# Four layers of a graph network on one core: eight sums per batch moved from GpSimd to VectorE

## The chip, the cores and the metric

The kernel runs on one core of a Trainium2 chip. The metric is the device time of one execution in microseconds (us). The core has TensorE (PE) for matrix products, VectorE (DVE) and GpSimd (POOL) for elementwise work, ScalarE (ACT) for activations and copies, and SyncE (SP), whose queue issues nearly all transfers here. Each engine takes its instructions in order and waits at an instruction until what it needs has been signalled.

## The reference

For each of 32 independent batches there are 512 nodes with 128 features, x, and a 512x512 matrix adj. Four layers follow each other. Each first normalises x over its features, applies relu, and adds the layer's result to x. Cut to what matters:

```python
h = max(layernorm(x), 0);  x = x + L0(h, adj)     # scaled adj + eye, one product, leaky relu
h = max(layernorm(x), 0);  x = x + L1(h, adj)     # adj @ in_rep and adj.T @ out_rep, tanh
h = max(layernorm(x), 0);  x = x + L2(h, adj)
h = max(layernorm(x), 0);  x = x + L3(h, adj)     # one product with adj, then gates

# L2 repeats this layer four times, on the same adj:
src_agg = einsum('bjv,bij->biv', nodes @ ws + bs, l2norm(adj, axis=2))
dst_agg = einsum('bjv,bji->biv', nodes @ wd + bd, l2norm(adj, axis=1))
out = tanh(concat([src_agg, nodes @ wn + bn, dst_agg]) @ wu + bu)
```

All arrays are fp32.

## The kernel before

**Tiles.** A matrix lies in SBUF as 128 partitions x 4 chunks x 512 columns. Each batch holds it twice: `a` is adj, `aT` its transpose, both loaded by SP. Layers 0 and 1 use them as they are. For layer 2 both are scaled in place: eight multiplications `L1100` per batch (four chunks of `aT`, four of `a`) with the inverse norms, which arrive by a transfer in `rows`.

**Seven products in place of eight.** In layer 2 every product with a scaled matrix is formed from blocks of half its size in the manner of Winograd's variant of Strassen's scheme: seven block products and some sums in place of eight block products. On the side of the matrices the sums are made once a batch for all four inner layers. That is `made_of(m)`, called for `aT` and for `a`: four subtractions each, on operands of 128 partitions x 2 x 256 elements. Three write the new tile `made` (parts 1, 0 and 2), one overwrites half of the chunks 0 and 2 of the matrix itself, so it must follow the part 1 that reads the old ones. These eight subtractions per batch are the ones that the change moves. All go through the helper `summed`, whose one line, L777, records them together with other sums: `st` (on the side of the features), and `p`, `to`, `de`, `ge`, which combine products in PSUM. The profile's groups are told apart by tiles, not by that line.

**Order.** Nothing is issued in the order of the text. Every operation is recorded with its engine, an estimate of its duration, and what it reads and writes. `Plan.order` then replays them: for each engine it takes, of the operations that are ready, the one with the smallest key (a due time from the batch's number less the longest path behind the operation), and the result is the fixed order of each engine's queue. The third argument of `summed` is that estimate; in the part that the change touches it is 1.6 us, for GpSimd. `kept_warm` then puts filler products (`ps_idle`) into TensorE's queue where the planned gap is over 0.7 us. Two or three batches are under way at once, so that one's layer 2 fills TensorE while others pass through their chains.

**Names that the steps use.**
- `sc` (L662): the power -1/2 of the variance, on GpSimd; `nb` (L670), on VectorE, follows it; `h` (L674), on ACT, is the normalised input.
- `inv` (L1081): the same power for the inverse norms of layer 2.
- `blk`, `turn_turned`, `turned`: a transposition over DRAM. VectorE transposes blocks of 32x32 (L683), SP writes four pieces (L692) and reads them back (L696). ACT makes `hT` or `f` of it (L730), or VectorE adds it to x (`xr`, L711). Batches 0, 1 and 31 transpose on TensorE instead (`ps_t`; `xr` is L708 there).
- `ps_agg`: products of unscaled matrices; `ps_sd`: the two projections of an inner layer, which VectorE moves to `sd` (L763), whereupon `st` is formed; `ps_ab`, `ps_cd`: the products of inner layers 0, 2 and 3; `ps_a`, `ps_b`, `ps_c`: those of inner layer 1, combined into `ge`, which `ps_second` multiplies; `ps_msg`: layer 3's first product, of `hT`.
- `t_sb` (L441): ten differences of weight columns, once, in the start.

Of the kernel before, what the change touches and what calls it, by code (L numbers as in the profile page):

```python
# [19 lines left out]
B, N, D = 32, 512, 128  # L20
# [261 lines left out]
def gnn_stack(  # L282
# [11 lines left out]
    nc = tc.nc  # L294
# [27 lines left out]
    def t_tt(n, pointers=0):  # L322
        return 0.065 + 0.058 * pointers + n / 960
# [13 lines left out]
    def op(*args, **kwargs):  # L337
        return plan.op(*args, **kwargs)
# [118 lines left out]
    def program(b):  # L457
        plan.batch = b

        def buf(tag, shape=(P, N), name=None):  # L460
            return plan.buf(tag, shape, name)
# [311 lines left out]
        def two(m, k, j):  # L773
            return lambda: m.ap().rearrange("p (q k) n -> p q k n", k=2)[:, :, k, j * H:(j + 1) * H]

        def summed(engine, eng, us, o, x, y, sign, reads, writes):
            op(engine, us, lambda: eng.tensor_tensor(o(), x(), y(), op=ALU.subtract if sign < 0 else ALU.add), reads, writes)  # L777
# [4 lines left out]
        def made_of(m):  # L782


            tm, even, odd = buf("s6", (P, 2, 3, H), "made"), {0, 2}, {1, 3}

            def t(k):
                return lambda: tm.ap()[:, :, k, :]

            for o, x, y, reads, writes in (  # L790
                    (t(1), two(m, 1, 1), two(m, 0, 1), [m], [(tm, {1})]),
                    (two(m, 0, 1), two(m, 0, 1), two(m, 0, 0), [(m, even)], [(m, even)]),
                    (t(0), two(m, 1, 1), two(m, 0, 1), [m], [(tm, {0})]),
                    (t(2), two(m, 1, 0), t(0), [(m, odd), (tm, {0})], [(tm, {2})])):
                summed("POOL", nc.gpsimd, 1.6, o, x, y, -1, reads, writes)
            return tm

        def right(m, tm, k, pair):
# [227 lines left out]
        z, y = buf("s2", name="z"), buf("s2", name="y")  # L1026
# [79 lines left out]
        f = f0  # L1106

        made = [made_of(m) for m in (aT, a)]
        for i, (wsd, wn) in enumerate(W_L2):
            f_new = buf("s2", name=f"f{i + 1}")  # L1110
# [99 lines left out]
```

## Time and profile before

| what | us |
|---|---|
| median of 3 runs | 2358.41 |
| lowest and highest of them | 2356.08, 2361.54 |
| the profiled execution | 2359.71 |
| its span in the profile | 2357.9 |

| engine | busy, us | share of the span |
|---|---|---|
| TensorE | 2275.6 | 97% |
| VectorE | 1810.0 | 77% |
| ScalarE | 1183.5 | 50% |
| GpSimd | 562.4 | 24% |

The busy time of an engine is an average over stages. A group of the profile reads: line, engine, operation, output<-inputs, shape, count; then busy us and mean ns of one; then the engine's idle time before these instructions and what ended most of it. Each product of 512 columns appears as four records of TensorE, since it is issued in two halves of 64 columns and each half is recorded twice. The granted TensorE clock is 0.996 of full speed.

The eight sums appear as six groups on GpSimd, 256 instructions with 358.7 us of busy time in all; the shortest of them lasts 1256 ns.

### The profile page before, as it was taken

The numbers are of one execution on the slowest core, as the hardware profiler recorded it, in microseconds if no ns is written. First come the engines' busy times: TensorE is split into PE (matmuls) and PEld (weight loads), VectorE is DVE, ScalarE is ACT, GpSimd is POOL, SyncE is SP. The second block draws the span as 40 slices with busy tenths as digits, with TensorE's granted clock in tenths as the row PEclk, the third lists the DMA queues.
The fourth block names the chain that finished last, engine by engine and source line by source line (L and its number), as shares of the span: only waits on it lengthen the run. The fifth ranks groups of instructions, "written<-read, shape, count | busy, mean of one in ns | idle before, by whom it ended". The sixth has DMA issues, their size and how long they took to land.

```text
span 2357.9 us, 48190 instructions
## 1 busy us (share of the span) xinstructions
PE 2275.6 (97%) x18380; PEld 1403.2 (60%) x18380; DVE 1810.0 (77%) x4592; ACT 1183.5 (50%) x2723; POOL 562.4 (24%) x459
## 2 busy tenths in 40 slices
PE   8999999999999999999999999999999999999999
PEld 6566665555655566655556655565555566555566
DVE  7766777888777878787877778887778787878664
ACT  6543555544555444555445555445555445554323
POOL 3321222222122221222221222221222212222200
PEclk9999999999999999999999999999999999999999
DMA  6121343444343444333443434433434443333211
GB/s 241 37 82 51 112 125 107 125 132 120 101 121 109 134 123 124 110 118 112 129 120 106 129 103 129 131 118 103 122 110 133 123 124 109 117 109 114 72 47 58
DMA packets 199144, 264.48 MB, mean 112 GB/s; under 512 B 25984, under 2 KB 130688, under 8 KB 198912
## 3 DMA queue, kind: packets, MB, share of 16 engines
q1 hardware_dynamic: 198624, 261.26, 36.9%
q8 instruction: 145, 2.38, 0.4%
q14 instruction: 87, 0.71, 0.1%
q10 hardware_dynamic: 288, 0.13, 0.0%
HBM read 199.18 MB, written 62.13 MB: 111 GB/s over the span
## 4 chain that ended last, share of the span: by engine, by line
PE 61%; DVE 22%; DMA 7%; issue 3%; ACT 3%; POOL 2%; SPq 1%; DVEq 0%; ACTq 0%; POOLq 0%
PE ps_ab L823 20%; PE ps_cd L823 13%; PE ps_agg L354 8%; PE ps_sd L354 7%; DMA turned<-turn_turned 4%; DVE a L1100 4%; PE ps_seven L354 4%; DVE aT L1100 3%; DVE ge L777 3%; PE ps_gate L354 2%; PE ps_second L354 2%; PE ps_msg L354 1%; DVE st L777 1%; DMA turn_turned<-blk 1%; POOL sc L662 1%
## 5 line engine op out<-in xcount | busy, mean ns | idle before, releaser
L823 PE MATMUL ps_ab<-made,st 128*64 128x256 f32 x1536 | 412.2, 382 | 1.6 <-DVE st L777 1.6
L777 POOL TENSOR_TENSOR made<-aT 128x512 f32<-128x512 f32 x64 | 93.2, 1457 | 948.0 <-DVE aT L1100 835.6
L662 POOL TENSOR_TENSOR sc<-v,neg_half 128x4 f32<-128x4 f32 x127 | 148.7, 1177 | 547.9 <-DVE v L623 372.3
L354 PE MATMUL ps_sd<-w_sb,f 128*64 128x256 f32 x2048 | 265.8, 379 | 0.0
L823 PE MATMUL ps_ab<-aT,sd 128*64 128x256 f32 x768 | 226.5, 383 | 0.0
L823 PE MATMUL ps_cd<-aT,st 128*64 128x256 f32 x768 | 223.7, 381 | 1.4 <-DVE st L777 1.4
L823 PE MATMUL ps_ab<-a,sd 128*64 128x256 f32 x768 | 225.0, 381 | 0.0
L823 PE MATMUL ps_cd<-a,st 128*64 128x256 f32 x768 | 221.4, 383 | 0.0
L823 PEld LDWEIGHTS ps_ab<-made,st 128*64 128x64 f32 x1536 | 209.1, 138 | 12.5 <-DVE st L777 2.5
L354 PEld LDWEIGHTS ps_sd<-w_sb,f 128*64 128x64 f32 x2048 | 164.8, 137 | 68.6 <-issue 16.4
L674 ACT ACTIVATE h<-xr,nb,sc 128x128 f32<-128x128 f32 x384 | 162.3, 486 | 80.4 <-DVE nb L670 80.3
L823 PE MATMUL ps_ab<-made,sd 128*64 128x256 f32 x768 | 198.7, 381 | 0.0
L823 PE MATMUL ps_ab<-f,w_sb 128*64 128x256 f32 x768 | 190.1, 379 | 0.0
L886 ACT ACTIVATE f<-to,cf_sb 64x512 f32<-64x512 f32 x192 | 117.7, 613 | 142.8 <-DVE to L777 142.5
L763 DVE TENSOR_TENSOR sd<-ps_sd,rf_sb 128x512 f32<-128x512 f32 x192 | 123.6, 684 | 76.0 <-PE ps_sd L354 75.8
L823 PE MATMUL ps_ab<-ge,w_sb 128*64 128x256 f32 x512 | 144.0, 383 | 3.8 <-ACT f L886 1.6
L823 PEld LDWEIGHTS ps_ab<-aT,sd 128*64 128x64 f32 x768 | 105.4, 138 | 70.3 <-issue 27.7
L354 PE MATMUL ps_agg<-aT,rep 128*64 128x512 f32 x512 | 141.3, 598 | 1.3 <-DVE rep L1053 1.2
L354 PE MATMUL ps_agg<-a,rep 128*64 128x512 f32 x512 | 140.6, 592 | 0.0
L777 DVE TENSOR_TENSOR p<-p,ps_ab 64x256 f32<-64x256 f32 x192 | 81.3, 423 | 71.0 <-PE ps_ab L823 43.7
L1100 DVE TENSOR_TENSOR a<-a,rows 128x512 f32<-128x512 f32 x128 | 134.6, 1070 | 0.9 <-PE ps_agg L354 0.9
L354 PE MATMUL ps_agg<-aT,msg 128*64 128x512 f32 (+1 forms) x528 | 126.7, 580 | 0.0
(218 smaller groups left out, 5974.5 us busy)
## 6 DMA issues: line engine op xcount, KB each, us to landing
aT<-in_adjt SPq DMA_DIRECT2D x124, 512.0 KB, 7.0
turn_turned<-blk SPq DMA_DIRECT2D x696, 64.0 KB, 1.8
turned<-turn_turned SPq DMA_DIRECT2D x174, 256.0 KB, 2.7
a<-in_adj SPq DMA_DIRECT2D x62, 512.0 KB, 3.9
rows<-bounce SPq DMA_DIRECT2D x32, 512.0 KB, 4.5
shares<-bounce SPq DMA_DIRECT2D x32, 512.0 KB, 4.2
x<-in_x SPq DMA_DIRECT2D x32, 256.0 KB, 9.0
out<-xr SPq DMA_DIRECT2D x31, 256.0 KB, 3.2
```

Of the source, the lines that this page charges most:

```text
L354: nc.tensor.matmul(to[c], weight[:, c], data, start=start, stop=stop, skip_group_check=True)
L662: op("POOL", t_pow(n), lambda: nc.gpsimd.tensor_tensor(inv.ap()[:, :n], v8.ap()[:, :n], neg_half[:, :n], op=ALU.pow), [v8, NH], [(inv, {0})])
L674: op("ACT", t_act(D, 2), lambda c=c: nc.scalar.activation(h.ap()[:, c, :], xin.ap()[:, c, :], AF.Relu, bias=nb.ap()[:, c:c + 1], scale=inv ...
L763: op("DVE", t_tt(N), lambda ps=ps, h=h: nc.vector.tensor_add(sd.ap()[:, 2 * h:2 * h + 2, :], ps.ap().rearrange("p (j v) -> p j v", j=2), a ...
L777: op(engine, us, lambda: eng.tensor_tensor(o(), x(), y(), op=ALU.subtract if sign < 0 else ALU.add), reads, writes)
L823: nc.tensor.matmul(to(), lhs(), rhs(), start=start, stop=True, skip_group_check=True)
L886: op("ACT", t_act(n, 1), lambda: nc.scalar.activation(f_new.ap()[rows, cols], src(), AF.Tanh, bias=cf_sb[rows, i:i + 1]), reads + [(CF, {i ...
L1100: op("DVE", t_tt(N), lambda m=m, c=c, s=s: nc.vector.tensor_mul(m.ap()[:, c, :], m.ap()[:, c, :], rows.ap()[:, s, :]), [(m, {c}), rows], [ ...
```

## The change

The loop of `made_of` hands its four subtractions to VectorE's queue instead of GpSimd's, and the planner is given VectorE's estimate for one operation of 512 elements, `t_tt(N)`, 0.065 + 512/960 = 0.598 us, in place of 1.6. Operands and the loop's order are the same. As the planner works out all queues anew, other instructions change their places too.

```diff
             for o, x, y, reads, writes in (
                     (t(1), two(m, 1, 1), two(m, 0, 1), [m], [(tm, {1})]),
                     (two(m, 0, 1), two(m, 0, 1), two(m, 0, 0), [(m, even)], [(m, even)]),
                     (t(0), two(m, 1, 1), two(m, 0, 1), [m], [(tm, {0})]),
                     (t(2), two(m, 1, 0), t(0), [(m, odd), (tm, {0})], [(tm, {2})])):
-                summed("POOL", nc.gpsimd, 1.6, o, x, y, -1, reads, writes)
+                summed("DVE", nc.vector, t_tt(N), o, x, y, -1, reads, writes)
             return tm
```

## The prediction

> **What bounds the kernel now.** I read the shares first, then the waits of TensorE, then the two stretches in which its waits lie.
>
> ```profile
> PE 2275.6 (97%) x18380; PEld 1403.2 (60%) x18380; DVE 1810.0 (77%) x4592; ACT 1183.5 (50%) x2723; POOL 562.4 (24%) x459
> ```
>
> TensorE is busy 2275.6 of 2357.9 us. Time can only come out of its 82 us of idle time and of the filler products (ps_idle)[...]. The waits of TensorE (line, what it waited for: us in total, times, longest) place most of that:
>
> ```profile
> PE ps_msg L354 <- ACT hT L730: 39.2, 27, 2.6
> PE ps_second L354 <- DVE ge L777: 20.2, 28, 0.9
> PE ps_idle L354 <- DVE xr L708: 6.0, 1, 6.0
> ```
>
> The first two come once a batch: 1.45 + 0.72 = 2.2 us of a period of 70.8 us (L1100 aT starts at 1219.11 and again at 1289.94). The third is one stall in the start. The groups of VectorE, each shape apart, show something odd about the operation beside the sums:
>
> ```profile
> L1100 DVE TENSOR_TENSOR a<-a,rows 128x512 f32<-128x512 f32 x128 | 134.6, 1070 | 0.9 <-PE ps_agg L354 0.9
> L1100 DVE TENSOR_TENSOR aT<-aT,rows 128x512 f32<-128x512 f32 x128 | 86.5, 680 | 2.5 <-DMA rows<-bounce 1.4 <-PE ps_agg L354 1.0
> ```
>
> The same operation on the same shape takes 680 ns for aT and 1070 ns for a. The a ones run while GpSimd works on sums of aT. The timelines of GpSimd and VectorE around 1226 us show it (start, us, what):
>
> ```profile
> 1226.35 1.61 POOL L777 TENSOR_TENSOR aT<-aT 128x512 f32<-128x512 f32 x1
> ...
> 1225.53 2.98 DVE L1100 TENSOR_TENSOR a<-a,rows 128x512 f32<-128x512 f32 x2
> ...
> 1232.95 1.22 DVE L670 SCALAR_TENSOR_TENSOR nb<-mv,sc 128x4 f32<-128x4 f32 x1 [0.40 <-POOL sc L662]
> ...
> 1235.65 1.94 PE L354 MATMUL ps_second<-ge,w_sb 128*64 128x512 f32 x8 [0.70 <-DVE ge L777]
> ```
>
> Two multiplications that should start 0.60 us apart take 2.9 us, and a 128x4 operation with a median of 164 ns takes 1.22 us. VectorE is back to back from 1218.5 to 1236.7 but for that 0.40 us, so its loss reaches ge, and TensorE.
>
> In the start it is worse. The chain of waits over 20 to 70 us runs through the same victims:
>
> ```profile
> 37.59 4.57 DVE a L1100 x4
> 42.16 0.08 DVE v L991
> 42.24 6.68 DVE t_sb L441 x9
> ...
> 52.46 6.47 PE ps_idle L354 x72
> ```
>
> Nine 128x64 subtractions take 6.7 us beside the sums, where 128x128 ones of the same kind take 0.28 us each in the clear (L452 to L455).
>
> **What the Trainium skill says.** "SBUF — State Buffer", section "SBUF: two separate sides": VectorE with two SBUF inputs and a GpSimd operation that reads SBUF share a port pair under an exclusive lock; whoever starts first keeps it for the whole instruction, the other blocks. The trace agrees: one multiplication of a rises to at most 1770 ns, one sum on GpSimd lasts about 1270 ns, and the clean multiplication 680. "GPSIMD Engine Reference", section "Engine selection": two-input elementwise work is about 2x slower there than on VectorE. Here it is 1270 ns (clean) against 680. "VectorE: DVE Perf Modes", section "Why tensor_tensor can't do 2×_2P or 4×": an fp32 tensor_tensor has no fast mode, so I price a sum like a multiplication. The trace agrees for contiguous operands (680 ns, starts 0.60 us apart: four aT from 35.09 to 37.51); the sums' two runs of 256 are seen on no VectorE row, which I bound below.
>
> **The change part by part.** Per batch, eight sums of 128x512 leave GpSimd and enter VectorE.
>
> *Total load.* Added: 256 x 0.60 = 154 us of VectorE. Removed: the lock's loss, 128 x (1.070 - 0.680) = 50 us on a, 127 x (0.406 - 0.164) = 31 us on nb (L670), some 6 us on t_sb and 1 us on one y. VectorE goes from 1810 to about 1880 us, 80%. It does not become the bound as a whole; only the stretch counts. GpSimd keeps its powers (L662, L1081) and loses the queue before them. It issues no DMA. Loads of a and aT no longer wait for GpSimd before reusing a buffer; that was 1.3 us in the waits of SP, so nothing.
>
> *The start.* Before: L1100 begins at 35.09, and the first ps_sd<-f (layer 2) at 60.51. After, with the built program's order, in which the eight sums follow the multiplications at once and t_sb comes after:
>
> | step | ends at, us |
> |---|---|
> | aT and a, 8 x 0.60 | 39.9 |
> | 8 sums x 0.60 | 44.7 |
> | one t_sb, xr L708 | 45.6 |
> | 4 statistics, 4 aggregations, small ones | 47.1 |
> | power on GpSimd 1.0; meanwhile t_sb x7 and half of z; nb | 48.9 |
> | h on ACT, 4 x 0.40 | 50.5 |
> | turn on TensorE, copy on ACT | 51.4 |
> | ps_agg of batch 2 on TensorE, then ps_sd<-f | 52.6 |
>
> That is 7.9 us earlier, and 3.4 us of ps_agg that came after ps_sd<-f before now lie ahead of it (the order of TensorE shows both moves, and one filler group of 6 where groups of 36 and 8 stood). So 11.3 us less idle, of which I give back 1 us at the next step, where ps_cd waits for sd and st. **Start: -10 us**, bounds -5 and -13. As TensorE is full afterwards, what is saved here stays saved.
>
> *The steady batches.* The order repeats from about batch 5 to 29, 27 periods with its like around. In VectorE's queue six sums now stand ahead of blk<-h (the transpose that feeds hT) and two behind it. From 1225.53 to the end of blk<-h:
> - added: 6 x 0.60 = 3.6 us;
> - gone: 1.7 us on a (2.9 - 1.2), 1.1 us on nb (1.26 to the next start, against 0.16), 0.40 us waiting for GpSimd's power, which two sums and blk<-y now cover, and some 0.4 us of gaps between dependent neighbours that sums now separate;
> - sum: 3.6 - 3.6 = 0. blk<-h ends at about 1236.7, as before.
>
> What waits behind it on the SP queue is the read-back of turned (for y), which stands after the first two writes of blk<-h in both orders. So xr L711 (1240.94) does not move either, nor the sd and st after it (first st at about 1244.6).
>
> Two orders change. (1) ge: the first ps_second<-ge needs ge's half 0, finished by the third of four operations before, by the second now: 0.43 us earlier, so this stall falls from 0.70 to about 0.3. (2) TensorE: ps_msg stood first, waiting for hT; now ps_cd and ps_ab, 5 pairs x 0.43 = 2.2 us, stand ahead of it, and the first ps_cd waits for st instead. A wait takes the place of the one removed: ps_cd can start at about 1244.6, against 1245.01 before with a quarter of ps_msg (0.27) done by then. Gain over both stalls 0.15 to 0.2 us in the batch shown, whose waits sum to 1.82; the mean batch waits 2.2 us, the excess being hT's DMA, which the new order hides. I take **-0.3 us a batch, -8 us** in 27. Bounds: none of the waits left, -2.2; sums at 0.70 instead of 0.60, +0.3.
>
> The two sums behind blk<-h fill VectorE's 0.93 and 1.79 us waits for ps_second and turned; without that cover they would cost 1.2 us. made is first used at 1245.9, 8 us after the sums end. A later blk<-h of the next layer's h (behind z, y and xr now, about 1.9 us) still leaves f0 ready at about 1256, and ps_sd<-f takes it at 1257.3. Batches 30 and 31 and the end lose no wait that I price.
>
> Sum: -10 - 8 = -18 us on the profiled execution's 2359.7 (span 2357.9 and 1.8 around it), which stands 1.3 us over the median of 2358.4: 2341.
>
> **The rivals.**
> - *Only the start is won.* The stall at ps_cd takes all that ps_msg gave: -10, 2348. For it: blk<-h does not move. Against: ge's new order. Chance 0.20.
> - *VectorE gives it back: slower.* The stretch 1225 to 1237 is VectorE's bound, and each 0.1 us by which a sum is dearer delays ge and blk<-h by 0.6 us a batch. If the lock explained only half of the 2.8 us, the stretch would end 1.4 us later: 27 x 1.1 (after the 0.3) - 10 = +20, 2378. It decides from a net delay of 0.37 us a batch (10/27). For it: VectorE has no slack there. Against: aT is 680 ns in all 128 cases, and a's median is 685 with a long tail, as of blocking by chance of time. Chance 0.16, a third of it within 0.2%.
> - *Both waits vanish.* -10 - 27 x 2.2 = -69, 2290. Against: hT hangs on SP and DMA behind the same blk<-h. Chance 0.04.
> - *My forecast*, 2326 to 2346: 0.60.
>
> That the change does not do what it says can be excluded: the built order has the 256 sums on VectorE.
>
> **How the numbers follow.** The likeliest case gives 2341. Start bounds and steady bounds of +-0.4 us a batch make 2326 to 2355; beyond it lie most of the slower rival and the vanished waits. About 0.2%, 4.7 us, is what this measurement can tell from no change: faster 0.82 (forecast, start only, waits vanish, less the tail above 2353.7), same 0.07, slower 0.11.
>
> **What would show it.** Right: a<-a,rows at 680 like aT; nb near 164; made on VectorE at about 680 ns; ps_sd<-f near 52.6; TensorE's wait for ge about halved, for hT gone, and one for st in its place of under 1 us a batch. Wrong: sums over 750 ns, a still above 900, or waits for st, ge and sd together above 2.5 us a batch.

## The result and the profile after

The changed kernel takes 2339.05 us (median of 3 runs, 2338.88 to 2339.23) against 2358.41; the ratio is 0.9917, with a 95% interval of 0.9894 to 0.9939. Its profiled span is 2337.5 us, at a granted clock of 0.999. The page's shares:

```profile
PE 2273.1 (97%) x18304; PEld 1350.8 (58%) x18304; DVE 1839.8 (79%) x4848; ACT 1175.0 (50%) x2723; POOL 239.4 (10%) x203
```

TensorE does the same work but for 76 records of filler products; VectorE has 256 more instructions and only 30 us more busy time. The waits of TensorE (us in total, times, longest):

```profile
PE ps_cd L823 <- DVE st L777: 24.7, 27, 2.1
PE ps_second L354 <- DVE ge L777: 21.9, 27, 1.6
```

The wait of ps_msg for hT (39.2 us) is gone; one of ps_cd for st has taken its place; the wait for ge is still there (20.2 before). The groups of VectorE, each shape apart (busy us, mean ns of one, idle before):

```profile
L1100 DVE TENSOR_TENSOR a<-a,rows 128x512 f32<-128x512 f32 x128 | 86.4, 682 | 0.8 <-PE ps_agg L354 0.7
L1100 DVE TENSOR_TENSOR aT<-aT,rows 128x512 f32<-128x512 f32 x128 | 86.3, 680 | 1.5 <-PE ps_agg L354 0.9 <-DMA rows<-bounce 0.6
L777 DVE TENSOR_TENSOR made<-aT 128x512 f32<-128x512 f32 x64 | 43.7, 683 | 0.0
L670 DVE SCALAR_TENSOR_TENSOR nb<-mv,sc 128x4 f32<-128x4 f32 x127 | 20.3, 160 | 15.1 <-POOL sc L662 14.1
```

The multiplication of a has fallen from 1070 to 682 ns, the same as that of aT, and nb from 406 to 160. A sum lasts 683 ns, so its runs of 256 elements cost nothing extra.

**The start.** The timeline of VectorE from the last multiplications on (start, us, what):

```profile
38.98 2.66 DVE L1100 TENSOR_TENSOR a<-a,rows 128x512 f32<-128x512 f32 x4
41.55 0.68 DVE L777 TENSOR_TENSOR made<-aT 128x512 f32<-128x512 f32 x1
...
45.77 0.68 DVE L777 TENSOR_TENSOR made<-a,made 128x512 f32<-128x512 f32 x1
...
49.10 0.89 DVE L441 TENSOR_TENSOR t_sb<-w_sb 128x64 f32<-128x64 f32 x6
```

and that of TensorE:

```profile
54.77 2.33 PE L354 MATMUL ps_sd<-w_sb,f 128*64 128x256 f32 x20
```

Six subtractions t_sb take 0.89 us; nine took 6.68 before. The first ps_sd<-f starts 18.3 us after the first L1100 (36.52 in this run) instead of 25.4. Between 45 and 65 us TensorE's idle time and filler products come to 0.05 + 1.87 us, against 6.04 + 8.03 before: 12.2 us won.

**A steady batch.** VectorE in the dense stretch, from the variance v to nb; then GpSimd and TensorE:

```profile
1214.08 0.16 DVE L623 TENSOR_SCALAR v<-mv 128x4 f32<-128x4 f32 x1
1214.15 0.68 DVE L777 TENSOR_TENSOR made<-aT 128x512 f32<-128x512 f32 x1
1214.75 0.68 DVE L777 TENSOR_TENSOR a<-a 128x512 f32<-128x512 f32 x1
1215.35 0.70 DVE L683 STREAM_TRANSPOSE blk<-y 128x512 f32<-128x512 f32 x1
1216.33 0.16 DVE L670 SCALAR_TENSOR_TENSOR nb<-mv,sc 128x4 f32<-128x4 f32 x1 [0.28 <-POOL sc L662]
```

```profile
1214.32 1.98 POOL L662 TENSOR_TENSOR sc<-v,neg_half 128x4 f32<-128x4 f32 x1 [38.60 <-DVE v L623]
```

```profile
1218.13 1.97 PE L354 MATMUL ps_second<-ge,w_sb 128*64 128x512 f32 x8 [1.09 <-DVE ge L777]
...
1228.49 0.43 PE L823 MATMUL ps_cd<-aT,st 128*64 128x256 f32 x1 [2.07 <-DVE st L777]
```

Six sums stand in the stretch and nothing is stretched on VectorE. But the power on GpSimd, 1.01 us in the trace of before, takes 1.98 us here: two sums on VectorE lie beside it. The power has both inputs in SBUF, so this fits the same exclusion the other way round.

### The profile page after: what moved, and what is told of

Its sections match the earlier page's. It is cut to its first block, busy times and chain, and to the rows that moved or that the text cites. A ratio compares the mean times of both kernels' runs of the same rounds, so it can differ in the third digit from the quotient of the medians.

```text
span 2337.5 us, 47892 instructions
## 1 busy us (share of the span) xinstructions
PE 2273.1 (97%) x18304; PEld 1350.8 (58%) x18304; DVE 1839.8 (79%) x4848; ACT 1175.0 (50%) x2723; POOL 239.4 (10%) x203
## 3 DMA queue, kind: packets, MB, share of 16 engines
q1 hardware_dynamic: 198624, 261.26, 37.2%
## 4 chain that ended last, share of the span: by engine, by line
PE 50%; DVE 22%; DMA 6%; issue 2%; POOL 2%; SPq 1%; ACT 1%; DVEq 0%; ACTq 0%; POOLq 0%
PE ps_ab L823 19%; PE ps_cd L823 11%; PE ps_sd L354 7%; DMA turned<-turn_turned 5%; PE ps_agg L354 5%; PE ps_seven L354 4%; DVE ge L777 3%; PE ps_gate L354 2%; DVE made L777 2%; POOL sc L662 2%; DVE aT L1100 2%; DVE bn L620 2%; DVE blk L683 2%; DVE a L1100 1%; DVE xr L711 1%
## 5 line engine op out<-in xcount | busy, mean ns | idle before, releaser
L662 POOL TENSOR_TENSOR sc<-v,neg_half 128x4 f32<-128x4 f32 (+1 forms) x127 | 179.5, 1420 | 1831.1 <-DVE v L623 1787.3
L354 PE MATMUL ps_sd<-w_sb,f 128*64 128x256 f32 x2048 | 271.9, 381 | 2.5 <-ACT f L1114 0.9
L354 PEld LDWEIGHTS ps_sd<-w_sb,f 128*64 128x64 f32 x2048 | 153.7, 137 | 89.6 <-issue 17.2
L823 PEld LDWEIGHTS ps_cd<-aT,st 128*64 128x64 f32 x768 | 102.2, 137 | 68.5 <-DVE st L777 38.0
L354 PE MATMUL ps_agg<-aT,h 128*64 128x512 f32 (+3 forms) x520 | 124.3, 586 | 2.0 <-ACT h L647 2.0
L823 PEld LDWEIGHTS ps_ab<-a,sd 128*64 128x64 f32 x768 | 104.8, 137 | 36.9 <-issue 1.3
```

What stands on the lines that cost most here:

```text
L354: nc.tensor.matmul(to[c], weight[:, c], data, start=start, stop=stop, skip_group_check=True)
L662: op("POOL", t_pow(n), lambda: nc.gpsimd.tensor_tensor(inv.ap()[:, :n], v8.ap()[:, :n], neg_half[:, :n], op=ALU.pow), [v8, NH], [(inv, {0})])
L823: nc.tensor.matmul(to(), lhs(), rhs(), start=start, stop=True, skip_group_check=True)
```

## The experiments

Theory: the exclusion between GpSimd's sums and VectorE's operations is lifted, which is worth some 10 us in the start; in the steady batches the slots of the sums eat that gain, and what is won comes from the new order of the queues. Rivals: the gain is in the steady batches, or it comes from the engine and not from the order.

**Batch 0 alone, and all but batch 0.** Only the sums of batch 0 go to VectorE (first_only), or only the others (rest_only).

```diff
-                summed("DVE", nc.vector, t_tt(N), o, x, y, -1, reads, writes)
+                if b == 0:        # rest_only: if b:
+                    summed("DVE", nc.vector, t_tt(N), o, x, y, -1, reads, writes)
+                else:
+                    summed("POOL", nc.gpsimd, 1.6, o, x, y, -1, reads, writes)
```

> Sums of batch 0 on VectorE, all others on GpSimd as before. Theory (the shared lock): the nine t_sb fall from 6.7 to about 1.3 us and a<-a,rows of batch 0 to 0.68 us each, so the start gains about 12 us and nothing else changes: 2346 (2343 to 2350), with TensorE's waits for hT and ge as before (1.4 and 0.7 us a batch) and a at about 1070 ns in the later batches. Rival (the gain lies in the steady order of TensorE): no more than 3 us, 2355 or above.

Measured: 2345.77 us against 2355.92 of the kernel before beside it, ratio 0.9954 (0.9938 to 0.9970): -10.2 us.

> Sums of batch 0 on GpSimd as before, all others on VectorE. Theory: the start keeps its stall of 6 us before xr and its fillers, and a batch gains 0.2 to 0.4 us by the new order (wait for hT gone, one for st of about 1 us, ge as before): 5 to 10 us, 2349 to 2354. Rival (the steady batches carry the gain): 2340 to 2345.

Measured: 2350.00 us, ratio 0.9976 (0.9964 to 0.9988): -5.9 us. The two add up to -16.1, of the 19 that the whole change brings. So the start is more than half of the gain from one batch of 32. The six runs with batch 0 alone spread from 2340.0 to 2350.64 us; the part "Batch by batch" below tells why. The profiles fit: with batch 0 alone t_sb falls to 217 ns while a stays at 1058, and TensorE's waits for hT (37.2 us) and ge (20.7) stay; with the others alone t_sb stays at 760, a falls to 700, and the waits are those of the change (st 22.5, ge 23.2).

**The order of the change, with the sums still on GpSimd.** The planner is told VectorE and VectorE's duration, so that all queues but those two are in the order of the change; the instructions go to GpSimd.

```diff
-                summed("DVE", nc.vector, t_tt(N), o, x, y, -1, reads, writes)
+                summed("DVE", nc.gpsimd, t_tt(N), o, x, y, -1, reads, writes)
```

> The planner is told that the sums run on VectorE, as in the changed kernel, but they are issued to GpSimd: order of every other instruction as in the changed kernel, sums and lock as before. Theory: a rises again to about 1070 ns and t_sb or its neighbours in the start to over 400 ns. In the steady batches the lock's loss of 2.8 us stands in the place of six sums of 3.6 us, so TensorE's waits are like those of the changed kernel or a little less; the start loses some 5 to 8 us of its gain, since GpSimd takes 10 us for what VectorE does in 4.9: 2342 to 2350. Rival (order alone makes the gain, the engine does not matter): 2339, start included. Second rival (GpSimd's powers queued behind its sums make the loss): nb late, TensorE's waits for st and ge above 2.5 us a batch, over 2360.

Measured: 2334.55 us (2332.91 to 2338.14), ratio 0.9910 (0.9897 to 0.9923): faster than expected, and not slower than the change itself. Its waits of TensorE:

```profile
PE ps_cd L823 <- DVE st L777: 32.3, 27, 2.8
PE ps_second L354 <- DVE ge L777: 6.7, 25, 0.7
PE ps_agg L354 <- ACT h L674: 5.4, 1, 5.4
```

The wait for ge is a third of that of the change. In this order the exclusion costs VectorE less than the sums do: in the stretch around 1215 us one multiplication of a (1.30 us), xr (1.76) and nb (1.22) lose 2.8 us together, and six sums take 3.6. The third line is where GpSimd loses: in the start the power stands behind eight sums in its queue. t_sb (248 ns) is mostly spared, since in this order seven of the nine here stand behind an operation that waits for that power. So VectorE's speed is not what helps the steady batches; the plan is, and with the sums on GpSimd it helps more (table below).

**Sums held back behind st.** From batch 3 on, all eight sums of a batch may start only after the last st of inner layer 2 of the batch before (late8_st), or only the last two of each matrix, parts 0 and 2 of made (late4_st, with `and n > 1`). They are not needed until some 25 us later.

```diff
+                past = [PAST["st", 2, b - 1]] if b > 2 else []
-                summed("DVE", nc.vector, t_tt(N), o, x, y, -1, reads, writes)
+                summed("DVE", nc.vector, t_tt(N), o, x, y, -1, reads, writes, past)
```

> The changed kernel, with the sums of a batch (from batch 3 on) held back in the plan until the last st of the inner layer 2 of the batch before, out of the dense stretch of VectorE; made is first needed some 15 us after that. Theory (what waits are left come from VectorE's dense stretch): the wait for ge falls from 0.8 to under 0.2 us a batch, those for st and hT together to about 0.7: 28 x 1.0, 2311 (2300 to 2322). Rival 1 (the wait for st and hT hangs on the transfers alone): ge vanishes, the other stays near 1 us: 2318 to 2325. Rival 2 (the sums collide with p, msg and z further on): no faster than 2339.

Measured: 2315.17 us (2314.3 to 2316.7), ratio 0.9826 (0.9813 to 0.9839). This beats both kernels.

> The change, with the last four of a batch's eight sums (made part 1 and part 2) held back, from batch 3 on, behind the last st of inner layer 2 of the batch before; the first four stay in the dense stretch. In the built order four sums instead of six stand ahead of the last ge (two ahead of the first pair), and none between ge and f2p. Theory (each sum in the stretch in front of ge and of blk<-h moves TensorE's wait by its own slot): with all six in the stretch TensorE waited 21.9 us for ge, with none 1.0; two of six taken out brings the ge wait to about 10 us (6 to 15), and the time lies between the two: 2325 us (2317 to 2332). Rival (only the sums that stand behind the ge pairs, or the order of TensorE, made the gain of the kernel with all eight held back): the time is that of the change, 2336 to 2341, or already that of the other, 2315.

Measured: 2322.70 us (2321.34 to 2323.56), ratio 0.9843 (0.9827 to 0.9858). The waits of TensorE, first with all eight held back, then with four:

```profile
PE ps_msg L356 <- ACT hT L732: 26.1, 27, 2.0
PE ps_second L356 <- DVE ge L779: 1.0, 3, 0.4
```

```profile
PE ps_msg L356 <- ACT hT L732: 37.9, 27, 2.4
PE ps_second L356 <- DVE ge L779: 5.3, 8, 1.4
```

The wait for ge goes 21.9, 5.3, 1.0 us with six, four and no sums ahead of the last ge: it hangs on the slots of the sums in the stretch. It falls faster than the count (about 10 us was expected with four). The time does not follow it: batches at full clock are as long with four sums ahead as with none (70.45 and 70.47 us, table below). What late4_st is slower by lies mostly at half clock and in the end: from f2p of batch 29 to the end its profile has 195.1 us against 190.4. ps_msg comes first again in both orders and waits for hT, which also brings TensorE to ge later; the runs don't part the two.

**The same order, sums on GpSimd.** As late8_st, with `nc.gpsimd` for `nc.vector`.

> The kernel with the sums held back until st, its order kept, the sums issued to GpSimd. Theory (what counts in the steady batches is that neither sums nor lock fall into the dense stretch before ge and blk<-h; a loss further on is covered by VectorE's waits there): steady waits as with the sums on VectorE, the start 7 us longer since the power waits behind the sums: 2322 (2316 to 2330). Rival (the lock hurts wherever it falls): over 2335.

Measured: 2422.56 us, ratio 1.0267 (1.0246 to 1.0288); late8_st's order has lost 107 us by the engine alone. The timeline of VectorE there, while sums run on GpSimd from 1267.45 to 1278.3:

```profile
1267.51 1.22 DVE L672 SCALAR_TENSOR_TENSOR nb<-mv,sc 128x4 f32<-128x4 f32 x1
1268.66 1.83 DVE L779 TENSOR_TENSOR st<-sd 128x256 f32<-128x256 f32 x2
1270.40 1.49 DVE L779 TENSOR_TENSOR st<-st,sd 128x256 f32<-128x256 f32 x1
1271.82 1.49 DVE L489 TENSOR_TENSOR s<-hT 128x256 f32<-128x256 f32 x1
1273.23 1.49 DVE L779 TENSOR_TENSOR st<-sd,st 128x256 f32<-128x256 f32 x1
1274.64 0.34 DVE L1033 SCALAR_TENSOR_TENSOR z<-ps_lin,sc,r_sb 128x128 f32<-128x128 f32 x1
```

With the sums on VectorE, st and s of this size take 0.42 us (0.76 for the first two). Here five operations in a row (nb, one of the first two st, and the next three) lose about 1.07 us each, and ps_cd and ps_ab wait for these st: 17.1 and 32.0 us over the run, with 18.4 more of ps_ab for f. All waits of TensorE sum to 102.7 us, 34.9 in late8_st; the rest of the 107 is 39 us more of its busy time, of which the granted clock, 0.994 against 1.000, would make some 15; the rest was not followed. In the steady batches no power is late: nb waits 37.3 us for sc, 36.0 in late8_st. In the start the power does stand behind the sums, and batch 2 comes 11.5 us later (table below). So in the steady batches this pair prices the exclusion by itself, and the price depends on what lies beside the sums: 2.8 us a batch where the planner put a, xr and nb beside them, some 5 to 6 where it put st, s, nb and y.

**Does a GpSimd operation that reads SBUF block, or any busy GpSimd?** Into the changed kernel, after the first sum of each matrix: four subtractions of made on GpSimd into a spare tile (lock_back), or ten memsets of that tile behind a 128x4 subtraction (memset_back), of about the same busy time, 340 and 336 us (and 34 of the small subtractions). The spare tile is used nowhere.

```diff
+                    for _ in range(4 * (n == 0)):      # memset_back: 10 times nc.gpsimd.memset(spare, 0.0)
+                        nc.gpsimd.tensor_tensor(spare..., t(1)(), t(1)(), op=ALU.subtract)
```

> The changed kernel and its order, with eight more subtractions per batch on GpSimd: four follow the first sum of each matrix, read that sum twice and write a spare tile that nobody reads. Nobody waits for them but the power behind them in GpSimd's queue. Theory (shared lock): VectorE's sums, a<-a,rows and nb in that stretch rise well above 680 and 164 ns, VectorE loses 3 to 8 us a batch there, and TensorE's waits grow by about that: 2420 to 2560. Rival (no lock; the a of before were slow for another reason): a and the sums stay at 680, 2336 to 2345.

> As the kernel with eight more subtractions on GpSimd, but with ten memsets of the spare tile for each matrix instead, behind one 128x4 subtraction that holds them until the first sum: GpSimd is busy about as long, writing without reading. Theory (the lock stands only against a GpSimd operation that reads SBUF): a and the sums at 680 ns, 2336 to 2346. Rival (any GpSimd operation blocks): as slow as the other, over 2400.

Measured: 2565.88 us (ratio 1.0883, 1.0856 to 1.0910) and 2566.17 us (1.0882, 1.0860 to 1.0903). The same time, but not for the reason under test. The groups of VectorE, first lock_back, then memset_back:

```profile
L1105 DVE TENSOR_TENSOR a<-a,rows 128x512 f32<-128x512 f32 x128 | 110.0, 867 | 0.7 <-PE ps_agg L355 0.7
L797 DVE TENSOR_TENSOR aT<-aT 128x512 f32<-128x512 f32 x32 | 45.4, 1418 | 0.0
L671 DVE SCALAR_TENSOR_TENSOR nb<-mv,sc 128x4 f32<-128x4 f32 x127 | 21.2, 167 | 134.9 <-POOL sc L663 133.9
```

```profile
L1107 DVE TENSOR_TENSOR a<-a,rows 128x512 f32<-128x512 f32 x128 | 86.6, 683 | 0.7 <-PE ps_agg L355 0.7
L797 DVE TENSOR_TENSOR aT<-aT 128x512 f32<-128x512 f32 x32 | 21.9, 684 | 0.0
L671 DVE SCALAR_TENSOR_TENSOR nb<-mv,sc 128x4 f32<-128x4 f32 x127 | 20.4, 160 | 195.1 <-POOL sc L663 194.1
```

The durations answer the question: beside reading subtractions the sum aT<-aT takes 1418 ns, beside memsets 684. The times don't: in both kernels the power sc, in order behind some 5 us of added work per matrix, comes late, and TensorE waits 162 and 179 us for ge, at a granted clock of 0.960 and 0.957. The pair can't price the exclusion; the pair before it does.

**Held back behind ge instead.** `PAST["ge", b - 1]`, from batch 3 on.

> The change, with all eight sums held back, from batch 3 on, behind the last ge of the batch before (not behind st): in the built order six follow blk<-h and stand in front of xr, sd and st, and ps_msg comes behind all twenty-four ps_sd and in front of ps_cd. Theory: what costs is a sum in front of ge, blk<-h or st. So the ge wait is gone (under 3 us), ps_msg's wait for hT too (under 8 us, since it now stands 1.3 us later and nothing is in front of blk<-h), and a wait for st comes back in part, as the six sums add 3.6 us in front of it: 5 to 25 us. Time 2315 us (2303 to 2328). Rival (any sums inside the stretch from ge to st cost the same, wherever they stand): 2335 to 2342, with a st wait over 25 us.

Measured: 2338.15 us (2335.45 to 2342.60), ratio 0.9914 (0.9892 to 0.9937). As the change, not 2315. The wait for ge is gone as expected (2.8 us), and the one for st didn't come (1.3); but others came:

```profile
PE ps_msg L356 <- ACT hT L732: 21.1, 27, 2.4
PE ps_sd L356 <- ACT f L1119: 14.9, 27, 0.9
PE ps_ab L826 <- ACT f L890: 10.8, 28, 0.6
```

The plan has a third order of TensorE, and stalls at f that no other kernel here has to this extent. Both the theory's time and the rival's reason (a st wait) missed. Which instruction of the new order makes f late was not followed further: open.

**The change once more** in the second comparison:

> The changed kernel itself, on the chip of these runs, to compare with: 2339 (2335 to 2343).

Measured: 2338.86 us (2337.86 to 2339.76), ratio 0.9916 (0.9897 to 0.9935). The result repeats.

**Batch by batch.** The start of f2p (L980 before, once a batch) cuts every profiled execution into batches. When batch 2 reaches it tells what the start has won. For batches 3 to 28 the table gives the mean length from one f2p to the next, apart for those in which TensorE's granted clock stays full and those in which it falls to half of full speed for 3.4 us or more.

| profiled execution | f2p of batch 2 at, us | at full clock | with a stretch at half clock |
|---|---|---|---|
| before | 226.8 | 22 of 71.21 us | 4 of 73.83 us |
| the change | 216.8 | 25 of 71.26 | 1 of 73.62 |
| the change once more | 215.2 | 26 of 71.37 | none |
| first_only | 218.3 | 24 of 71.23 | 2 of 73.89 |
| rest_only | 225.0 | 25 of 71.21 | 1 of 73.51 |
| planned_dve_on_pool | 226.1 | 24 of 70.57 | 2 of 73.77 |
| late8_st | 213.9 | 26 of 70.47 | none |
| late4_st | 215.0 | 24 of 70.45 | 2 of 72.52 |
| late8_ge | 215.6 | 25 of 71.17 | 1 of 73.86 |
| late8_st_on_pool | 225.4 | 23 of 73.40 | 3 of 75.33 |

The standard error of a mean at full clock is 0.1 to 0.2 us. One of the four stretches of before, first the wait ahead of it, then the stretch in a view of windows (us, busy us of TensorE, granted clock, share of DMA, GB/s):

```profile
1388.07 0.44 PE L354 MATMUL ps_msg<-w_sb,hT 128*64 128x128 f32 x4 [2.63 <-ACT hT L730]
...
1388.50:1391.90 3.40, 3.40 (x20) 0.50 0.15 31
```

Batches at full clock have not become shorter by the change. What it wins in the steady batches is three stretches at half clock fewer, or four in the repetition; a batch with one is 2.6 us longer (1.7 for the half clock, the rest mostly the longer wait). Batches 3 to 28 together take 1861.9 us before, 1855.1 and 1855.5 after. Each of the four stretches before (from 600.0, 1101.7, 1388.5 and 2101.8 us) comes with a wait of ps_msg for hT of 2.3 to 2.6 us, the one after (1229.6) with the wait of 2.07 us for st shown above. That a long single wait brings it on is likely from this but not tested; one of 2.31 us before passed without. The other executions agree: before, the time falls from 2361.8 us at a granted clock of 0.995 (mean of four) to 2348.48 at 0.999 (one). The latter is 10 us above the changed kernel at the same clock, about what the start alone wins.

## Why the prediction was right, and where it was not

Predicted were 2341 us and -18; measured are 2339.05 and -19. The start came as reckoned. The steady batches brought about the amount that was forecast, but not in the way forecast: that the amount agrees is luck.

- **The exclusion.** Right: a at 682 ns like aT, nb at 160, t_sb from 759 to 216. The Trainium skill's page "SBUF — State Buffer", section "SBUF: two separate sides", says that a VectorE operation with two SBUF inputs is held up only by GpSimd operations that read SBUF; the memset pair agrees (684 against 1418 ns).
- **The price of a sum.** Right: 683 ns, most starts 0.60 us apart.
- **The load of VectorE.** 1880 us predicted, 1839.8 measured. The losses gone are as reckoned (48 us on a, 31 on nb, 5 on t_sb). The term that is too large is the 154 us added: short operations that stood apart now overlap with the sums between them (v takes 0.07 us to the next start in the stretch, 0.18 before). I have not added that up over the whole run. It did not matter, as the total was no bound.
- **The start.** -10 predicted, of which 11.3 less idle and 1.0 given back at ps_cd. Measured 12.2 less idle and fillers, all told; first_only shows -10.2 in time, and batch 2 comes 9.9 us earlier. ps_sd<-f came 18.3 us after L1100 instead of 17.5 (at 54.77 us and not 52.6, as L1100 itself began 1.4 us later). The order alone does not bring this: with it and the sums on GpSimd, batch 2 comes at 226.1 us, against 226.8 before. How much of it is the exclusion (a and t_sb take some 7.4 us less on VectorE) and how much the shorter run of the sums, no run parts.
- **The steady batches, sum: right by luck.** -8 predicted; rest_only shows -5.9, and the whole change less first_only about -9. But it is not 0.3 us in each batch: at full clock a batch takes 71.26 us, 71.21 before. That the new order hides hT's longest waits was right; priced was their idle time alone. The waits per batch went from 2.16 us to 1.77 (330 to 2100 us: hT 34.3 and ge 18.3 before; st 23.1 and ge 19.5 after), in part because the longest ones are gone.
- **A term put at nothing: the clock.** "Time can only come out of its 82 us of idle time and of the filler products" left out the stretches at half clock, though the granted clock of before, 0.996, was known. Fewer of them are what the steady batches won.
- **The steady batches, step (2): right.** st's wait came where hT's was, 0.92 us a batch; "under 1 us" was predicted.
- **The steady batches, step (1): wrong.** ge's wait was to fall from 0.70 to 0.3 us; it rose to 0.81 in the mean, 1.09 in the batch shown. The order did what was said: ps_second starts after the second ge, not the third. The failed term is the balance "3.6 - 3.6 = 0". From the first operation of the stretch to blk<-h are 10.84 us now (1208.07 to 1218.91) and 10.46 before (1225.53 to 1235.99), 0.38 more. The sums take 3.71. On a 1.68 is gone, on nb 1.18, in gaps 0.35: about as predicted. But of the 0.40 us wait for the power only 0.12 is gone, since the power now takes 1.98 us beside two sums. I had looked at the exclusion from VectorE's side alone. The other part is that TensorE no longer stands at ps_msg for hT, so it is earlier at ps_second relative to VectorE; how the rise divides between the two no run tells.
- **A wrong reading that did no harm.** "made is first used at 1245.9, 8 us after the sums end" took the made of the batch before for this batch's own, which is used some 25 us later. The conclusion (covered) holds all the more, and that slack is what late8_st uses for another 24 us.
- **The rivals.** "VectorE gives it back" was placed rightly: the stretch is VectorE's bound, and the wait for ge that remains is its doing. The net delay was 0.38 us, against the 0.37 it gave as its turning point. That it did not decide fits the new order, which had taken ps_msg's wait away; the point was reckoned with that wait in front of everything. "Only the start is won" was given 0.20, and it describes the batches at full clock.

Nor was it foreseen that in the steady batches the move itself costs: with the order of the change and the sums on GpSimd the kernel is as fast (2334.55), since 0.7 us less in a batch at full clock (70.57 against 71.26) makes up for a start that wins nothing.

## What to carry to other kernels

Before moving work to a faster engine, ask which stretch its new slots lie in: eight sums shorten no batch at full clock when they enter a full stretch of VectorE, and each by 0.7 us when they wait some 20 us for a freer one, with the same instructions. Where two engines exclude each other, price it in both directions and for the small operations, since a 128x4 operation loses as much as a large one. Compare the granted clocks before a few us are put down to waits: here most of what the steady batches won lay in them. And when a planner sets the order, run the new order with the old engine too: it tells what the engine brought and what the plan did.

## What the runs showed of the hardware

- The exclusion works both ways: in the changed kernel 26 of the 97 powers of 128x4 on GpSimd take 1.9 to 2.1 us beside sums on VectorE; before, 94 of 97 lie between 0.9 and 1.05 us. In late8_st, where the sums lie elsewhere, one is that long.
- On VectorE it strikes operations with both inputs in SBUF, whatever their size: beside the sums of late8_st_on_pool nb (128x4) goes from 147 to 1221 ns and st (128x256) from 416 to about 1490, medians. Operations with one input in PSUM are not touched: p<-p,ps_ab takes 423 ns there and 424 in the clear, z<-ps_lin 342 and 342. Nor are block transposes (696 and 711 ns).
- A memset of 128x512 on GpSimd takes 525 ns and holds up no VectorE operation with two inputs (a<-a,rows 684 ns beside them, 683 in the clear). One with a single input it does: v<-mv (128x4) takes 610 ns when it starts beside memsets and 160 in the clear, medians. And as GpSimd works in order, 5 us of it ahead of a 1 us power made TensorE lose some 6 us a batch (179 us in 27 waits).
- A stretch at half clock lasts 3.4 us in most cases here. In the one at 1229.6 us after, the products of each half (128x256) start 0.42 to 0.43 us apart, before and behind it 0.21 to 0.22.
